# One kernel of four chained layers: layer 2's expert combination taken up in every second round, two products of its keys made by one set of matmuls, and layer 3's weights loaded during layer 2

## The chip, the cores and the metric

The kernel runs on one core of one Trainium2 chip. A core has five engines with a queue each: PE (TensorE: matrix products; the loads of their weights have a row of their own, PEld), DVE (VectorE), ACT (ScalarE), POOL (GpSimd) and SP (SyncE, which here only starts transfers). They meet through semaphores, and each works through its own queue. The metric is the device time of one execution in microseconds (us), as the median of several runs. Beside it there is one profiled execution, from which every instruction's start and duration are known; spans of instructions are taken from that one.

## What is computed

An input of 8 sequences of 512 positions by 128 channels goes through four layers. Each layer normalises x, puts it through an attention-like block (s) and a feed-forward block (ffn), and adds s * silu(ffn) to x. The change touches layers 2 and 3. Cut to what matters:

```python
# layer 2, s: a gated delta rule over positions (4 heads, 32 key and 64 value channels per head)
def _step(S, inp):
    q_t, k_t, v_t, g_t, b_t = inp
    S = S * jnp.exp(g_t)[..., None, None]
    v_eff = (v_t - jnp.einsum('bhk,bhkv->bhv', k_t, S)) * b_t[..., None]
    S = S + k_t[..., None] * v_eff[..., None, :]
    o_t = jnp.einsum('bhk,bhkv->bhv', q_t, S)
    return (S, o_t)
# layer 2, ffn: 8 experts with a capacity of 640 tokens, each token sent to its best two
h = jax.nn.relu(jnp.einsum('ecd,edh->ech', xin, w1) + b1[:, None, :])
out = jnp.einsum('ech,ehd->ecd', h, w2) + b2[:, None, :]
out = out * jnp.where(valid, tok_w, 0.0)[:, :, None]
final = jnp.zeros((S + 1, d), xf.dtype).at[idx.reshape(-1)].add(out.reshape(-1, d))[:S]
# layer 3, s: causal attention, 16 heads of 64, with a position bias; q = x @ Wq and so on, out @ Wo + bo
logits = logits + causal[None, None] + _pos_bias(rel_pos_bias, T)[None]
probs = jax.nn.softmax(logits / dh, axis=-1)
# layer 3, ffn: whole-number weights over 127
h = jax.nn.silu(gate) * up
return jnp.einsum('bsh,dh->bsd', h, wd)
```

## The kernel before

**Order of the work.** The order of PE is written out by hand, by Python generators that are stepped in rounds (`step` takes a generator on to its next `yield`). The instructions of the other engines are put into each queue by the framework that builds the program, which can set an instruction ahead of others that the code writes earlier; dependencies, buffers and semaphores come from it as well. A tile's `tag` names a set of buffers, and `bufs` how many there are; a new tile of a tag waits until the oldest of its buffers is free. Pools are laid on one another: a pool that is opened after another was closed gets its memory.

**Layer 2** (`layer2`, L1043 and on) works on eight units u = 0 to 7 (half of the sequences q, a quarter of the positions t). For each unit four generators run side by side in twelve rounds (`rounds`, L1047): `delta_scan` of u (the recurrence, four chunks of three rounds: pk and rhs; pu and U; pn, po and the new state stn), `delta_inverse` of u + 1 (the triangular inverse of each 32x32 block of key products), `delta_front` of u + 2 (norm, convolution py, scaling, the transposes `chan`) and `delta_output` of u - 1 (named `out`). The inverse makes AT (keys by keys, L1497 to L1507) and PT (keys by queries) from `KT` and the two halves of `chan[1]`, each by 64 groups of 32x32 tiles, and multiplies each by the decay matrix E; AO (POOL, L1515), TT and TM follow from AT, and then four levels of PE products pY and pU.

Beside these run the experts (`experts2`): seven steps each, eight experts, one or two steps in a round, from u = 1 on; they end in round 6 of u = 4. Their outputs go to a DRAM buffer `l2eo_d`. When they are through, `combine2` (L1369) takes the units one by one in two steps. The first loads the unit's s again (`sr`, L1376, from SP), issues eight indirect loads of expert rows (`g<-l2eo_d`, L1311, from POOL: four of the best expert's rows into a tile of tag `xin`, four of the second's into one of tag `eo`, two buffers each) and multiplies both by their weights on DVE (L1384). The second adds them (L1388), takes the tanh on ACT (L1389), multiplies (L1390, L1391) and adds to x on POOL (L1394). It has no PE instruction. It is stepped in every round with u > 3 (L1062). `sr` and the output's `s_sb` (L1676) share the tag `s`, two buffers. Unit 7's combination comes after the last round, as its s is the last to be made.

**Layer 3** (`layer3`, L1684) opens its pools when layer 2's are closed. It loads Wv, Wq and Wk (L194, 512 KB each), the position bias (four DVE memsets L1905 and four loads L1906, 512 KB each), Wo (L194), a small bias (L1695), and the three whole-number weights, which `dequantised` (L1909) turns into transposed floats: a load of 192 KB, a cast (L1917) and a scaling (L1918) on DVE, three PE transposes (L1921) and a copy. All loads are issued by SP. In PE's order the nine transposes stand ahead of layer 3's first own product: the transposes of the first normalised sequence (`ptxnT`), then `pv`, the values from Wv.

The scan step that sets the pace in the later units, in the code's words:

```python
for h in range(4):
    tiles32(pk[:, h, :], r["KT"][:, ch, h, :], st[:, h, :])
...
U = wk.tile([P, 4, 64], F32, tag="U", name=f"U{nm}", bufs=2)
A.copy(U, pu)
...
V.tensor_tensor(new, new, pn, ALU.add)
```

Of the kernel before, what the change touches and what calls it, by code (L numbers as in the profile page):

```python
# [31 lines left out]
def tile_kernel(ctx: ExitStack, tc: tile.TileContext, w: dict, out: bass.AP):  # L32
# [6 lines left out]
    sm = ctx.enter_context(tc.tile_pool(name="sm", bufs=4))  # L39
    fw = sm2 = None  # L40
    keep = ctx.enter_context(tc.tile_pool(name="keep", bufs=1, space=bass.MemoryType.DRAM))
# [985 lines left out]
    def layer2():  # L1027
        nonlocal wk, fw, sm2
        with ExitStack() as lx:
# [9 lines left out]
            with tc.manual_schedule(engines={mybir.EngineType.PE}):  # L1039
                front = delta_front(0, c)  # L1040
                step(front)
                loaded2(c)
                N = 2 * NT  # L1043
                out = iter(())

                def rounds(u, experts, combined, n_experts):
                    nonlocal out  # L1047
                    scan = delta_scan(u, c)
                    inverse = delta_inverse(u + 1, c) if u + 1 < N else iter(())
                    front = delta_front(u + 2, c) if u + 2 < N else iter(())  # L1050
                    for r in range(12):
                        step(scan)
                        step(experts)
                        if not u and r > 1:
                            step(experts)
                        step(inverse)
                        if r > 1:
                            step(front)
                        if r % 3 < n_experts:
                            step(experts)  # L1060
                        step(out)
                        if u > 3:  # L1062
                            step(combined)
                    drain(scan, inverse, front, out)
                    out = delta_output(u, c)

                with tc.tile_pool(name="route2", bufs=1) as rp:
                    routed = route2(rp, c)
                    drain(front)
                    front = delta_front(1, c)  # L1070
                    for _ in delta_inverse(0, c):
                        step(front)
                    drain(front)
                    rounds(0, routed, iter(()), 0)
                    drain(routed)
                with tc.tile_pool(name="ex2", bufs=1) as ep:
                    experts = experts2(ep, c)
                    combined = combine2(ep, c)
                    for u in range(1, N):
                        rounds(u, experts, combined, 1)  # L1080
                    drain(out, experts, combined)

# [320 lines left out]
    def delta_front(u, c):  # L1403
# [20 lines left out]
        for back in range(4):  # L1424
            x = wk.tile([P, 4, P], F32, tag=f"nb{back}", name=f"nb{back}{nm}", bufs=1 if back else 4)
            for s in range(4):
# [11 lines left out]

        y = wk.tile([P, 4, S], F32, tag="y", name=f"y{nm}", bufs=1)
        for ch in range(4):  # L1440
# [34 lines left out]
        for i, parts in enumerate((((0, None, G), (1, gam, V)), ((0, beta, G), (1, None, V)))):  # L1475
            byt = wk.tile([P, 2, 4, 4, 32], F32, tag="byt", name=f"byt{i}{nm}", bufs=1)
            for k, part in enumerate(parts):
                scaled(byt[:, k], *part)
            x = wk.tile([P, 2, 4, 4, 32], F32, tag=f"chan{i}", name=f"chan{i}{nm}", bufs=1 if i else 3)
            V.transpose(x.rearrange("p a c h i -> p (a c h i)"), byt.rearrange("p a c h k -> p (a c h k)"))  # L1480
# [8 lines left out]
    def delta_inverse(u, c):  # L1489
# [6 lines left out]

        prod = []  # L1497
        for i, n in enumerate(("AT", "PT")):
            pp = psS.tile([P, 4, 4, 32], F32, tag="S", name=f"p{n}{nm}")
            for ch in range(4):  # L1500
                for h in range(4):
                    tiles32(pp[:, ch, h, :], r["KT"][:, ch, h, :], chan[1][:, i, ch, h, :])
            x = wk.tile([P, 16, 32], F32, tag=n, name=f"{n}{nm}", bufs=1 + i)
            V.tensor_tensor(x, pp.rearrange("p c h i -> p (c h) i"), E, ALU.mult)
            prod.append(x)
            yield
        AT, r["PT"] = prod  # L1507

# [14 lines left out]
        def flipped(n):  # L1523
            x = wk.tile([P, 16, 32], F32, tag="TM", name=f"TM{nm}_{n}", bufs=1)
            V.transpose(x.rearrange("p n i -> p (n i)"), TT.rearrange("p n i -> p (n i)"))
# [4 lines left out]
        for n in range(1, 5):  # L1530
            pp = psS.tile([P, 16, 32], F32, tag="S", name=f"pY{nm}_{n}")
            for i in range(16):
                tiles32(pp[:, i, :], ao[n][:, i, :], TM[:, i, :])
            Y = wk.tile([P, 16, 32], F32, tag="Y", name=f"Y{nm}_{n}", bufs=1)
            A.copy(Y, pp)
# [50 lines left out]
    def decay_pairs(u, g, c):  # L1586

        gl = wk.tile([P, 16, 32], F32, tag="gl", name=f"gl{u}", bufs=1)
        G.tensor_tensor(gl, bcast(c["leb"], 1, 16), bcast(g, 2, 32), ALU.mult)
        pd = psS.tile([P, S], F32, tag="S", name=f"pd{u}")  # L1590
        mm(pd, c["gt32"], gl.rearrange("p n i -> p (n i)"))
        E = wk.tile([P, 16, 32], F32, tag="E", name=f"E{u}", bufs=1)
        A.activation(E.rearrange("p n i -> p (n i)"), pd, AF.Exp)
# [88 lines left out]
    def layer3():  # L1682
        nonlocal wk
        with ExitStack() as lx:  # L1684
            lp = lx.enter_context(tc.tile_pool(name="l3", bufs=1))
            wk = lx.enter_context(tc.tile_pool(name="wk3", bufs=2))
            c = dict(lp=lp, xnT={}, v={}, qk={}, P={}, PT={}, th={}, s={})
            for n in "vqk":
                c["w" + n] = loaded(lp, [P, 1024], w[f"L3_attn_W{n}"], f"l3w{n}")
            c["bias"] = position_bias(lp, shared["bias"])  # L1690
            c["wo"] = loaded(lp, [P, 8, D], w["L3_attn_Wo"].rearrange("(g p) o -> p g o", p=P), "l3wo")
            G.tensor_scalar(c["wq"], c["wq"], 1.0 / 64.0, 0.0, ALU.mult, ALU.add)
            bo = lp.tile([1, NT, D], F32, name="l3bo")
# [5 lines left out]
            c["one"] = one  # L1699
            c["gT"], c["uT"], c["dT"] = (dequantised(lp, w[f"L3_ffn_w_{n}"], n) for n in ("gate", "up", "down"))  # L1700

# [206 lines left out]

    def dequantised(pool, src, name):  # L1909

        raw = pool.tile([P, 3, P], I32, tag="rawi", name=f"rawi{name}")
        if src.shape[0] == P:
            nc.sync.dma_start(raw, src.rearrange("o (c p) -> o c p", p=P))
        else:
            nc.sync.dma_start(raw, src.rearrange("(c p) d -> p c d", p=P))
        f = pool.tile([P, 3, P], F32, tag="rawf", name=f"rawf{name}")
        V.tensor_copy(f, raw)  # L1917
        V.tensor_scalar(f, f, 1.0 / 127.0, None, ALU.mult)  # L1918
        pt = psS.tile([P, S], F32, tag="S", name=f"pti{name}")
        for k in range(3):  # L1920
            T.transpose(pt[:, k * P : (k + 1) * P], f[:, k, :], ident)  # L1921
        dst = pool.tile([P, 3, P], F32, name=f"l3{name}")
        evac(dst, pt[:, 0 : 3 * P].rearrange("p (c o) -> p c o", o=P))
        return dst

    with tc.tile_pool(name="x12", bufs=1) as x12:
        with tc.tile_pool(name="fw", bufs=8) as fw:
            layers01()
        layer2()
    layer3()  # L1930


# [21 lines left out]
```

## Time and profile before

| | |
|---|---|
| median of 3 runs | 4039.8 us (4029.34 to 4045.39) |
| the profiled execution | 4008.45 us, span 4006.7 us |
| PE busy over the span | 89% |
| layer 2, from its first convolution product to the last s | 2423 to 3161 us |
| layer 3, from its first `pv` to the end | 3192.55 to 4006.7 us |
| granted TensorE clock, mean | 0.933 |
| indirect loads of the combination, `g<-l2eo_d` | 64, of 0.944 us (median) on POOL |

The time is that of one core, so an engine's busy time counts only where the others wait for it. The profile lists, for each idle stretch of an engine, what ended it (the releaser), and follows the chain of work that ended last back from the end. "Issue" stands for time in which an engine waited for nothing that the profile shows. Times in windows are counted from the span's start. In layers 0, 1 and 3 PE is busy in nine tenths of nearly every slice; in layer 2 (slices 24 to 32 of 40) it is busy in four to nine tenths.

### The profile page before, as it was taken

The page shows a single profiled execution, that of the slowest core. Times are in us where ns is not written, and L with a number is a line of the kernel's source. Part 1 is how long each engine was busy: PE and PEld are TensorE (multiplying, and loading weights), DVE is VectorE, ACT ScalarE, POOL GpSimd, SP SyncE. Part 2 cuts the span into 40 slices and gives each one's busy share as a digit, 9 for nine tenths or more (in the row PEclk, how much of TensorE's full clock was granted, in tenths as well). Part 3 has the DMA queues.
Part 4 walks back from the last instruction along what each step waited for, and adds up shares of the span by engine and source line. Part 5 has one row for each costly group of instructions (what it writes and reads, how often), then busy time and mean ns, then how long its engine had stood idle before and what let it go on. Part 6 is the DMA issues. An engine that isn't in the chain of part 4 may idle for free. (4 is left out here: it accounts for less than half of the span.)

```text
span 4006.7 us, 87035 instructions
## 1 busy us (share of the span) xinstructions
PE 3580.8 (89%) x33646; PEld 1712.2 (43%) x33646; DVE 2268.1 (57%) x7301; ACT 1831.8 (46%) x3996; POOL 1470.8 (37%) x2122
## 2 busy tenths in 40 slices
PE   3899999999999999999999985788947599999998
PEld 1343344444344333333333333456635355555555
DVE  4655666665655544446446646544454466666665
ACT  1254454455454556565664641122211155555554
POOL 2233334334443333332333333444373133333333
PEclk6999999999999999999999987899967699999999
DMA  3000000000011232222222320011020200000000
GB/s 110 29 23 30 28 13 30 30 18 26 26 44 51 75 104 72 80 73 72 71 75 68 81 75 28 11 42 51 28 51 22 63 1 4 4 4 4 4 4 6
DMA packets 139420, 163.29 MB, mean 41 GB/s; under 512 B 30047, under 2 KB 79878, under 8 KB 138880
## 3 DMA queue, kind: packets, MB, share of 16 engines
q1 hardware_dynamic: 135680, 150.91, 13.2%
q0 software_dynamic: 3328, 6.82, 1.0%
q8 instruction: 266, 4.36, 0.5%
q14 instruction: 146, 1.20, 0.1%
HBM read 129.94 MB, written 30.08 MB: 40 GB/s over the span
## 5 line engine op out<-in xcount | busy, mean ns | idle before, releaser
L500 DVE CUSTOM_DVE_ANT_0 l0junk<-ps,l0junk 128x512 f32<-128x512 f32 (+3 forms) x1024 | 502.2, 490 | 394.1 <-PE ps L82 319.6
L985 POOL TENSOR_TENSOR h<-h,C 128x512 f32<-128x512 f32 x256 | 325.2, 1271 | 640.1 <-ACT h L983 587.0
L556 ACT ACTIVATE PT<-pt 128x512 f32<-128x512 f32 (+1 forms) x768 | 360.9, 524 | 404.7 <-PE ps L82 364.2
L807 DVE TENSOR_REDUCE nm<-ps 128x1 f32<-128x512 f32 x512 | 331.7, 685 | 327.2 <-PE ps L82 326.2
L1791 POOL TENSOR_SCALAR P<-P,l 128x128 f32<-128x128 f32 (+3 forms) x512 | 262.8, 532 | 537.8 <-DVE l L1789 382.4
L1788 ACT ACTIVATE P<-P,mx 128x128 f32<-128x128 f32 (+3 forms) x512 | 281.2, 550 | 300.0 <-DVE mx L1786 296.5
L82 PE MATMUL ps<-l0kA,l0qA 32*128 32x512 f32 (+3 forms) x2048 | 403.8, 479 | 11.4 <-DVE mx L500 11.4
L560 POOL TENSOR_SCALAR_AFFINE_SELECT PT<-PT 128x256 f32<-128x256 f32 x512 | 202.0, 407 | 518.9 <-ACT PT L556 486.7
L82 PE MATMUL pt<-l0qA,l0kA 32*128 32x512 f32 (+3 forms) x2048 | 373.2, 468 | 2.0 <-DVE nm L807 1.1
L82 PE MATMUL ps<-l1kA,l1qA 32*128 32x512 f32 x1024 | 332.0, 652 | 29.0 <-DVE nm L807 26.7
L845 ACT ACTIVATE PT<-pt 128x512 f32<-128x512 f32 x512 | 276.3, 595 | 176.0 <-PE ps L82 146.3
L82 PE MATMUL av<-PT,vl0v 128*9 128x512 f32 (+3 forms) x3072 | 319.4, 504 | 1.2 <-POOL PT L560 1.2
L82 PE MATMUL ph<-xnT,l1e 128*128 128x512 f32 x512 | 295.4, 660 | 7.2 <-DVE H L834 2.7
L982 ACT ACTIVATE h<-ph 128x512 f32<-128x512 f32 x272 | 162.8, 599 | 252.6 <-PE ph L82 227.0
L82 PE MATMUL pt<-l1qA,l1kA 32*128 32x512 f32 x1024 | 273.6, 644 | 1.0 <-DVE nm L807 1.0
L82 PE MATMUL po<-h,l1e 128*128 128x512 f32 x512 | 266.5, 602 | 0.0
L82 PEld LDWEIGHTS pt<-l0qA,l0kA 32*128 32x128 f32 x2048 | 165.3, 184 | 206.8 <-DVE mx L500 66.9
L1784 DVE CUSTOM_DVE_ANT_0 P<-ps,l3bias 128x128 f32<-128x128 f32 (+3 forms) x512 | 225.0, 486 | 41.2 <-PE ps L82 39.4
L649 POOL TENSOR_TENSOR h<-h,C 128x512 f32<-128x512 f32 x128 | 163.0, 1274 | 112.3 <-ACT h L647 64.3
L647 ACT ACTIVATE h<-ph,l0b 128x512 f32<-128x512 f32 x192 | 132.0, 687 | 127.6 <-PE ph L82 127.5
L82 PEld LDWEIGHTS ps<-l0kA,l0qA 32*128 32x128 f32 x2048 | 158.3, 187 | 48.3 <-DVE mx L500 34.7
L82 PE MATMUL ps<-kT,qT 64*128 64x128 f32 (+3 forms) x1024 | 176.0, 456 | 1.2 <-ACT kT L77 0.7
(522 smaller groups left out, 6424.5 us busy)
## 6 DMA issues: line engine op xcount, KB each, us to landing
C<-wd SPq DMA_DIRECT2D x288, 256.0 KB
qd<-qf SPq DMA_DIRECT2D x24, 256.0 KB
kd<-kf SPq DMA_DIRECT2D x24, 256.0 KB
l0qA<-qd SPq DMA_DIRECT2D x256, 16.0 KB
l0kA<-kd SPq DMA_DIRECT2D x256, 16.0 KB
l2e<-in_L_ffn_w_dram SPq DMA_DIRECT2D x16, 256.0 KB
l3flat<-l3short SPq DMA_DIRECT2D x16, 192.0 KB
l2eo_d<-eo SPq DMA_DIRECT2D x8, 320.0 KB
```

Source lines behind the costliest of these rows:

```text
L82: T.matmul(out_, lhsT, rhs, start=start, stop=stop)
L500: V.tensor_tensor_reduce(c["junk"][:, : (qb + 1) * P], pss[j][:, at], c["mask"][:, (3 - qb) * P :], 1.0, NEG, ALU.add, ALU.max, mx[i][:, q ...
L556: A.activation(p[:, j % 2, :N], pss[j][:, :N], AF.Exp)
L560: G.affine_select(out=own, in_=own, compare_op=ALU.is_ge, fill=0.0, base=0, pattern=[[0, 2], [1, P]], channel_multiplier=-1)
L649: G.tensor_tensor(h, h, C[b, e], ALU.mult)
L807: V.tensor_reduce(nm[g][:, j, qb : qb + 1], pss[j], AX.X, ALU.max, negate=True)
L845: A.activation(Pt[j // 2][:, j % 2, :], pss[j], AF.Exp)
L982: A.activation(h, ph, AF.Relu)
L985: G.tensor_tensor(h, h, C[b, u - u % 2][:, u % 2, :], ALU.mult)
L1784: V.tensor_tensor_reduce(p, src, c["bias"][:, 2 * g + j, (3 - qb) * P :], 1.0, NEG, ALU.add, ALU.max, mx[:, n : n + 1])
L1788: A.activation(p, p, AF.Exp, bias=mx[:, n : n + 1], accum_out=l[:, n : n + 1])
L1791: G.tensor_scalar(p, p, l[:, n : n + 1], 1.0, ALU.mult, ALU.mult)
```

## The change

It has three parts. `combine2` is stepped only in the odd rounds of u > 3. AT and PT are made together: `KT` is the stationary operand of one matmul per tile whose moving operand has both halves of `chan[1]` (64 columns instead of 32), in two halves of eight blocks, each followed by two DVE multiplications of 256 columns instead of one of 512; both products are whole after the second half. And a pool `wk23` (`wf`) is opened around both layers, into which ten of layer 2's tiles move; a generator `weights3`, stepped in every round of u = 7, loads layer 3's seven weights into those tiles' buffers (`y`, `byt`, `chan1`, `gl`, `E`, `nb1`) once layer 2 is through with them, scales Wq, and dequantises into `AT`, `TM` and `Y`. `layer3` takes them from there; the position bias and the small bias are loaded as before. The pool `x12` now stays open during layer 3.

```diff
...
@@ -1042,6 +1042,7 @@
                 loaded2(c)
                 N = 2 * NT
                 out = iter(())
+                weights = weights3()
 
                 def rounds(u, experts, combined, n_experts):
                     nonlocal out
@@ -1059,8 +1060,10 @@
                         if r % 3 < n_experts:
                             step(experts)
                         step(out)
-                        if u > 3:
+                        if u > 3 and r % 2:
                             step(combined)
+                        if u == N - 1:
+                            step(weights)
                     drain(scan, inverse, front, out)
                     out = delta_output(u, c)
 
@@ -1078,7 +1081,7 @@
                     combined = combine2(ep, c)
                     for u in range(1, N):
                         rounds(u, experts, combined, 1)
-                    drain(out, experts, combined)
+                    drain(out, experts, combined, weights)
 
     def masks2(lp):
 
@@ -1422,7 +1425,7 @@
 
         nb = []
         for back in range(4):
-            x = wk.tile([P, 4, P], F32, tag=f"nb{back}", name=f"nb{back}{nm}", bufs=1 if back else 4)
+            x = (wf if back == 1 else wk).tile([P, 4, P], F32, tag=f"nb{back}", name=f"nb{back}{nm}", bufs=1 if back else 4)
             for s in range(4):
                 (G.tensor_copy if s % 2 else A.copy)(x[:, :, 32 * s : 32 * s + 32],
                                                      nT[:, s, 3 - back : P + 3 - back].rearrange("p (c i) -> p c i", i=32))
...
@@ -1473,10 +1476,10 @@
 
         chan = r["chan"] = []
         for i, parts in enumerate((((0, None, G), (1, gam, V)), ((0, beta, G), (1, None, V)))):
-            byt = wk.tile([P, 2, 4, 4, 32], F32, tag="byt", name=f"byt{i}{nm}", bufs=1)
+            byt = wf.tile([P, 2, 4, 4, 32], F32, tag="byt", name=f"byt{i}{nm}", bufs=1)
             for k, part in enumerate(parts):
                 scaled(byt[:, k], *part)
-            x = wk.tile([P, 2, 4, 4, 32], F32, tag=f"chan{i}", name=f"chan{i}{nm}", bufs=1 if i else 3)
+            x = (wf if i else wk).tile([P, 2, 4, 4, 32], F32, tag=f"chan{i}", name=f"chan{i}{nm}", bufs=1 if i else 3)
             V.transpose(x.rearrange("p a c h i -> p (a c h i)"), byt.rearrange("p a c h k -> p (a c h k)"))
             chan.append(x)
         r["KT"], r["QgT"] = chan[0][:, 0], chan[0][:, 1]
@@ -1494,17 +1497,17 @@
         E = decay_pairs(u, r["g"], c)
         yield
 
-        prod = []
-        for i, n in enumerate(("AT", "PT")):
-            pp = psS.tile([P, 4, 4, 32], F32, tag="S", name=f"p{n}{nm}")
-            for ch in range(4):
-                for h in range(4):
-                    tiles32(pp[:, ch, h, :], r["KT"][:, ch, h, :], chan[1][:, i, ch, h, :])
-            x = wk.tile([P, 16, 32], F32, tag=n, name=f"{n}{nm}", bufs=1 + i)
-            V.tensor_tensor(x, pp.rearrange("p c h i -> p (c h) i"), E, ALU.mult)
-            prod.append(x)
-            yield
-        AT, r["PT"] = prod
+        AT = wf.tile([P, 16, 32], F32, tag="AT", name=f"AT{nm}")
+        r["PT"] = wk.tile([P, 16, 32], F32, tag="PT", name=f"PT{nm}", bufs=2)
+        for half in range(2):
+            pp = psS.tile([P, 8, 2, 32], F32, tag="S", name=f"pAP{nm}_{half}")
+            for n in range(8):
+                ch, h = divmod(8 * half + n, 4)
+                tiles32(pp[:, n, :, :], r["KT"][:, ch, h, :], chan[1][:, :, ch, h, :])
+            at = slice(8 * half, 8 * half + 8)
+            for i, x in enumerate((AT, r["PT"])):
+                V.tensor_tensor(x[:, at, :], pp[:, :, i, :], E[:, at, :], ALU.mult)
+            yield
 
         ao = []
 
...
@@ -1684,12 +1687,8 @@
         with ExitStack() as lx:
             lp = lx.enter_context(tc.tile_pool(name="l3", bufs=1))
             wk = lx.enter_context(tc.tile_pool(name="wk3", bufs=2))
-            c = dict(lp=lp, xnT={}, v={}, qk={}, P={}, PT={}, th={}, s={})
-            for n in "vqk":
-                c["w" + n] = loaded(lp, [P, 1024], w[f"L3_attn_W{n}"], f"l3w{n}")
+            c = dict(lp=lp, xnT={}, v={}, qk={}, P={}, PT={}, th={}, s={}, **shared["w3"])
             c["bias"] = position_bias(lp, shared["bias"])
-            c["wo"] = loaded(lp, [P, 8, D], w["L3_attn_Wo"].rearrange("(g p) o -> p g o", p=P), "l3wo")
-            G.tensor_scalar(c["wq"], c["wq"], 1.0 / 64.0, 0.0, ALU.mult, ALU.add)
             bo = lp.tile([1, NT, D], F32, name="l3bo")
             for t in range(NT):
                 nc.sync.dma_start(bo[:, t, :], w["L3_attn_bo"].rearrange("(o d) -> o d", o=1))
@@ -1697,7 +1696,6 @@
             one = lp.tile([1, P], F32, name="l3one")
             G.memset(one, 1.0)
             c["one"] = one
-            c["gT"], c["uT"], c["dT"] = (dequantised(lp, w[f"L3_ffn_w_{n}"], n) for n in ("gate", "up", "down"))
 
             groups = [(b, g) for b in range(B) for g in range(8)]
             n = 2 * len(groups)
@@ -1906,28 +1904,45 @@
             nc.sync.dma_start(bias[:, h : h + 4, 2 * P :], skewed[:, h : h + 4, P - 1 : 3 * P - 1])
         return bias
 
-    def dequantised(pool, src, name):
-
-        raw = pool.tile([P, 3, P], I32, tag="rawi", name=f"rawi{name}")
-        if src.shape[0] == P:
-            nc.sync.dma_start(raw, src.rearrange("o (c p) -> o c p", p=P))
-        else:
-            nc.sync.dma_start(raw, src.rearrange("(c p) d -> p c d", p=P))
-        f = pool.tile([P, 3, P], F32, tag="rawf", name=f"rawf{name}")
-        V.tensor_copy(f, raw)
-        V.tensor_scalar(f, f, 1.0 / 127.0, None, ALU.mult)
-        pt = psS.tile([P, S], F32, tag="S", name=f"pti{name}")
-        for k in range(3):
-            T.transpose(pt[:, k * P : (k + 1) * P], f[:, k, :], ident)
-        dst = pool.tile([P, 3, P], F32, name=f"l3{name}")
-        evac(dst, pt[:, 0 : 3 * P].rearrange("p (c o) -> p c o", o=P))
-        return dst
+    def weights3():
+
+
+        c = shared["w3"] = {}
+        two = wf.tile([P, 2, 1024], F32, tag="y", name="l3wvq")
+        c["wv"], c["wq"] = two[:, 0, :], two[:, 1, :]
+        c["wk"] = wf.tile([P, 1024], F32, tag="byt", name="l3wk")
+        for n in "vqk":
+            nc.sync.dma_start(c["w" + n], w[f"L3_attn_W{n}"])
+        c["wo"] = loaded(wf, [P, 8, D], w["L3_attn_Wo"].rearrange("(g p) o -> p g o", p=P), "l3wo", tag="chan1")
+        names = (("gate", "gT", "gl", "AT"), ("up", "uT", "E", "TM"), ("down", "dT", "nb1", "Y"))
+        raws = []
+        for n, _, tag, _ in names:
+            src = w[f"L3_ffn_w_{n}"]
+            raw = wf.tile([P, NT, P], F32, tag=tag, name=f"l3raw{n}")[:, 0:3, :]
+            nc.sync.dma_start(raw.bitcast(I32), src.rearrange("o (c p) -> o c p", p=P) if src.shape[0] == P else
+                              src.rearrange("(c p) d -> p c d", p=P))
+            raws.append(raw)
+        yield
+        G.tensor_scalar(c["wq"], c["wq"], 1.0 / 64.0, 0.0, ALU.mult, ALU.add)
+        for _ in range(3):
+            yield
+        for raw, (n, key, _, tag) in zip(raws, names):
+            V.tensor_copy(raw, raw.bitcast(I32))
+            V.tensor_scalar(raw, raw, 1.0 / 127.0, None, ALU.mult)
+            yield
+            pt = psS.tile([P, S], F32, tag="S", name=f"pti{n}")
+            for k in range(3):
+                T.transpose(pt[:, k * P : (k + 1) * P], raw[:, k, :], ident)
+            c[key] = wf.tile([P, NT, P], F32, tag=tag, name=f"l3{n}")[:, 0:3, :]
+            evac(c[key], pt[:, 0 : 3 * P].rearrange("p (c o) -> p c o", o=P))
+            yield
 
     with tc.tile_pool(name="x12", bufs=1) as x12:
         with tc.tile_pool(name="fw", bufs=8) as fw:
             layers01()
-        layer2()
-    layer3()
+        with tc.tile_pool(name="wk23", bufs=1) as wf:
+            layer2()
+            layer3()
 
 
 _OUT = (B, S, D)
```

The tiles `y`, `TM`, `Y`, `gl` and `E` are moved from `wk` to `wf` in the same way as `nb1`, `byt` and `chan1` above.

## The prediction

> **What bounds the kernel now.** I read the slices first, to see which stage leaves PE idle, then layer 2 unit by unit, then the waits in its worst unit, then the chain of waits where layer 2 hands over to layer 3. The slices:
>
> ```profile
> PE   3899999999999999999999985788947599999998
> DMA  3000000000011232222222320011020200000000
> ```
>
> Outside layer 2 and its end PE is at 8 or 9 tenths, so the change can only win in slices 24 to 32. Busy times in stretches from one unit's first U to the next one's (units 3, 4, 5, 6, 7), then from the last s product to layer 3's first `pv` (columns: stretch, its length, busy time and instructions of PE, weight loads, DVE, ACT, POOL, granted clock, DMA share, GB/s):
>
> ```profile
> 2783.15:2864.80 81.65, 74.71 (x2112) 54.92 (x2112) 40.64 (x112) 21.05 (x47) 29.45 (x33) 0.92 0.13 36
> 2864.80:2985.18 120.38, 67.52 (x2056) 47.06 (x2056) 57.23 (x141) 19.16 (x44) 83.20 (x95) 0.75 0.24 50
> 2985.18:3065.07 79.89, 59.33 (x2021) 43.66 (x2025) 43.48 (x117) 14.05 (x34) 31.85 (x38) 0.71 0.11 23
> 3065.07:3124.12 59.05, 39.45 (x1944) 33.34 (x1934) 27.36 (x60) 8.20 (x17) 17.35 (x19) 0.70 0.10 22
> 3124.12:3160.60 36.48, 23.92 (x600) 18.08 (x600) 22.04 (x99) 6.31 (x13) 6.67 (x8) 0.83 0.05 17
> 3160.60:3192.55 31.95, 3.54 (x14) 2.36 (x14) 13.11 (x41) 1.07 (x2) 2.95 (x6) 0.50 0.52 166
> ```
>
> Two places stand out. Unit 4 has less for PE than unit 3 (67.52 against 74.71 us) and takes 38.7 us more; POOL goes from 29.45 to 83.20. And in the last stretch PE works 3.54 of 31.95 us. DVE's waits from 2890 to 3000, in which unit 4's end lies (total, times, longest):
>
> ```profile
> DVE g L1384 <- DMA g<-l2eo_d,l2row: 28.1, 7, 6.6
> DVE st L109 <- POOL x L1394: 5.9, 2, 5.3
> DVE un L1459 <- POOL usq L1457: 5.2, 1, 5.2
> DVE g L1384 <- issue: 5.1, 1, 5.1
> ```
>
> DVE stands at the multiplications of gathered rows, and TM and rhs, which PE needs, stand behind them. In the same stretch POOL issues 56 of the 64 gathers, 1.25 us apart (0.94 and 0.30 of issue): 70 us. The second line tells more: `st L109` is layer 3's norm, the last work in the code, and runs in the middle of this burst. So whatever is ready is put into any gap, however late it stands in the code. At the handover the chain of waits reads (start, us, what):
>
> ```profile
> 3160.60 0.70 DVE s_sb L1676
> 3161.32 2.03 DMA l2s_d<-s_sb
> 3163.48 2.65 DMA sr<-l2s_d
> ...
> 3178.35 5.10 DMA rawigate<-in_L_ffn_w_gate_dram
> ...
> 3190.11 0.90 PE ptidown L1921 x3
> 3191.02 0.87 PE ptxnT L125 x4
> 3191.91 0.59 ACT xnT L77
> 3192.55 7.76 PE pv L82 x14
> ```
>
> The last combination ends at 3168.6. Then layer 3's loads queue on SP, the 192 KB weights last, and nine transposes that wait for them stand in PE's order ahead of `ptxnT`.
>
> **The change, part by part. Weights of layer 3.** Nothing that waits for these loads is left ahead of `ptxnT`. It then needs only the normalised sequence. The last x is added by 3168.6, the four memsets L1905 run from 3168.9 to 3173.0, the four `xn` (L118) follow at 3172.95 and take 0.93: 3173.88. Transposes to `pv` took 3190.60 to 3192.55 = 1.95 us; so `pv` starts near 3175.9 instead of 3192.55: **-16.65**. If the memsets went behind `xn` it would be 4 us more. Late next would be the position bias: its four loads were issued 3170.1 to 3171.7, its first use was at 3204.7 and would be at 3188. In the stretch 3170 to 3180 DMA moved 352 and 359 GB/s; 2.1 MB at that rate is 6 us, so it lands by about 3178, 10 us early.
>
> What is added to unit 7: on SP seven issues (0.33 to 0.5 us each), in front of loads and stores of the scan's output; SP was otherwise idle there, and all buffers loaded into were last used by unit 7's front (u = 5) or the start of its inverse (u = 6). On POOL 1.07 us (Wq). On DVE three times 0.36 + 0.36 and one or two copies of 0.56, on ACT the rest (0.48), on PE three times 0.9. Unit 7 waits in turn for PE, DVE and ACT (24 of 36 us PE busy), so a piece in the way costs its length at most: 3 x (0.72 + 0.9) = 4.9 us at worst, 0 if all fall into waits. I take **+2**. The dequantisation was 5.5 us of PE, DVE and copies at the handover; that is in the 16.65. If the raw weights are late, DVE stands there with the scan's rhs behind it: up to 5.1 us (the landing time above) for each of three.
>
> **One set of products.** 128 matmuls of 32 columns took 1.28 us at full clock (`pAT`, 2701.18 to 2702.47), 10 ns each; 32 of 64 columns (`pk`, 3128.32) 0.65 us, 20.3 ns each. Per unit 2 x 1.28 becomes 128 x 20.3 = 2.60: PE's work stays. Half of the instructions go: 1024 matmuls and 1024 weight loads in all. In the chain of waits from 2390 to 3230 "issue" has 9.7% of 840 = 81 us, over some 33,300 PE instructions 2.4 ns each: 2048 x 2.4 = **-5**. (For bounds: PE's idle time by issue ahead of `pPT` is 8.8 us in all, half is 4.4; weight loads' there 18.9, half 9.5; below, 0 if the same fetch is only met later.) The rows are those of the tile `pPT`:
>
> ```profile
> L82 PE MATMUL pPT<-chan,chan x1024: 184/194/258, 2461.0 to 3073.5; 32*32 32x32 f32 x171
>   issue: 18.9, 14
> ```
>
> [...]
>
> DVE gets four multiplications of 256 columns (`stn` L1628, from PSUM too: 0.41) for two of 512 (0.69): 1.64 - 1.38 = 0.26 us, eight times 2.1, half on the path: **+1**. AT is whole only a round later, where PT was before. From AT's end to pY: AO 1.27, TT 1.74, TM 0.70, 0.2 of gaps = 3.9. From PT's end to pY there were 5.3, 24, 8.2, 6.1, 9.6, 7.5, 3.3 and 4.1 us in units 0 to 7, so PE waits longer in unit 6 only (0.6) and has nothing to spare in unit 7: **+1**. Sum of this part -3, from -10 to +3.
>
> **Combination in every second round.** It takes no instruction away: 64 gathers of 1.25 us on POOL, 16 DVE multiplications, all the rest stays. What moves is where they stand in the code: units 0 to 3 were reached in rounds 6, 8, 10 of u = 4 and 0 of u = 5; now in 7, 11, 3 and 7. But the 56 gathers issued by 2992 are all of units 0 to 5 and half of 6 and 7, whose place is u = 6, u = 7 and after the last round: they go when the rows and a buffer are there. Both stay as they were for units 0 to 2. One thing does change by the buffers: tag `s` has two, given in the order of the code, and unit 4's `s_sb` (written at 3027) now comes ahead of unit 3's `sr`. So unit 3's second half leaves the burst, and with it eight gathers whose buffers it frees (four of unit 5, then four of unit 7). Of the last eight, four ran while POOL then waited anyway (1.09 us before `byt` at 2979.4), four held AO back from 2989.5 to 2992.55: 3.0 us; unit 3's `sr` on DVE (0.68) stood ahead of TT. They come back at 3027 and later, where POOL idled 17.6 us. I take **-4**. Bounds: if the burst dissolved, unit 4 would take its PE time and unit 3's idle time, 67.5 + 6.9 = 74.5: -46. If the two multiplications moved to u = 5 each stop DVE for the longest wait seen, 6.6: +13. The value is near the second end, since only an eighth of the gathers moves.
>
> **Sum.** -16.65 + 2 - 3 - 4 = **-21.7 us**, made against the profiled execution: 4008.45 gives 3986.8. That execution is 31 us shorter than the median; taken off the median of 4039.8 it is **4018**. The parts' bounds (loads -20.7 to -1.3 with three late casts; products -10 to +3; combination -46 to +13) leave most between 4000 and 4030.
>
> **Rivals.** *The burst dissolves.* For it: POOL has 40 us free between 3003 and 3100, and a unit's ten us of gathers every four rounds (about 25 us) would fit. Against it: the norm of layer 3 shows that place in the code doesn't hold ready work back. Time: -14.65 - 3 - 46: 3976. *The load's gain is lost to unit 7.* The casts are put where the weights are expected, and DVE stands there with rhs behind: 3 x 5.1 = 15.3 us; -21.7 + 15.3 = -6.4: 4033. For it: DVE did stand seven times for gathers expected earlier. Against: the buffers are free some twenty rounds ahead. *Slower: gathers land on the scan.* If units 3 to 6 move wholly into u = 5 to 7, where PE, DVE and ACT take turns and nothing hides a stop, their eight multiplications stop DVE 6.6 us each: 53, less what the burst loses by it, between 0 and their share of its waits, 4/7 of 28.1 + 5.1 = 19; in the middle +43, with -14.65 and -3 it is +26, or 4066. It decides from 17.65 us of net stops on. For it: the two multiplications outside the burst, at 3045 and 3112, cost DVE 8.9 us more of this wait. Against it: place in the code doesn't hold them, as before. *It doesn't do what it says:* loads are held back by a buffer until the handover; then 16.65 is lost and the sum is -5: 4035. I count this with the second.
>
> **How the numbers follow.** Forecast 0.55 (4005 to 4030), burst dissolved 0.15, gain lost 0.20, gathers on the scan 0.10. A measurement of this kernel tells about 0.5%, 20 us, from no change: 4019.6 is the border, and the forecast lies on it. Of its 0.55 about 0.38 falls beyond, with the first rival's 0.15 that makes faster 0.53; the second and the forecast's rest make no change 0.37; slower 0.10. The range reaches from the dissolved burst to near the slower case: 3974 to 4046.
>
> **What would show it.** `pv` 15 us or more sooner after the last x, with no `pti` between: the loads. First bias use without a wait on DMA: nothing is late next. POOL's gathers still 1.25 us apart for 40 to 48 in a row and DVE's wait for them near 25 us: the burst stands; under 10 us, it dissolved, and the prediction is wrong. `pPT`'s issue waits halved, no new wait of pY for TM in units 2 to 5. Unit 7 longer by more than 5 us would say that the casts come too early.

## The result, and the profile after

| | before | after |
|---|---|---|
| median of the compared runs | 4034.7 us (4 runs, 4029.3 to 4045.4) | 4000.7 us (4 runs, 3994.7 to 4005.5) |
| profiled execution, span | 4006.7 us | 3993.0 us |
| mean granted TensorE clock | 0.933 | 0.935 |

The ratio is 0.9912, 95% interval 0.9884 to 0.9939: faster by 0.9%, 34 us between the medians. Between the two profiled executions only 13.7 us lie; why is the first question below.

The slices of PE and of the DMA engines after:

```profile
PE   3899999999999999999999985689957699999998
DMA  3001000000011232222222211011122100000000
```

The weak slices of PE are the same as before, 24 to 32 of 40. Of the transfers, slice 32 had 2 tenths and has 1; slices 28 to 31 have 6 together instead of 3, as the loads now run during layer 2's last units. The same stretches as before, from one unit's first U to the next one's (units 3, 4, 5, 6, 7), and then from the last s product to layer 3's `pv` (stretch, length, busy time and instructions of PE, weight loads, DVE, ACT, POOL, granted clock, DMA share, GB/s):

```profile
2791.32:2870.21 78.89, 72.56 (x1984) 52.51 (x1985) 40.37 (x115) 21.18 (x47) 27.65 (x32) 0.96 0.12 34
2870.21:2995.22 125.01, 83.00 (x1940) 54.93 (x1944) 55.40 (x143) 19.28 (x43) 78.07 (x88) 0.71 0.20 45
2995.22:3071.23 76.01, 59.02 (x1884) 42.35 (x1878) 44.39 (x131) 14.56 (x35) 37.60 (x45) 0.77 0.24 49
3071.23:3127.45 56.22, 37.68 (x1820) 31.79 (x1810) 26.66 (x59) 8.20 (x16) 18.53 (x20) 0.77 0.18 47
3127.45:3164.47 37.02, 25.59 (x609) 19.25 (x609) 22.97 (x101) 6.79 (x14) 6.67 (x8) 0.82 0.05 17
3164.47:3179.10 14.63, 1.12 (x5) 0.72 (x5) 7.91 (x22) 0.58 (x1) 1.88 (x5) 0.50 0.51 160
```

The last stretch fell from 31.95 to 14.63 us. Unit 4 is still the long one, and longer than in the profile of before (125.01 against 120.38). The chain of waits over the handover after (start, us, what):

```profile
3164.47 0.70 DVE s_sb L1679
3165.19 1.99 DMA l2s_d<-s_sb
3167.32 2.58 DMA sr<-l2s_d
...
3172.66 0.91 DVE l3bias L1903
3173.73 0.91 DVE l3bias L1903
3174.80 0.91 DVE l3bias L1903
3175.88 0.91 DVE l3bias L1903
3176.79 0.34 DVE xn L118 x2
3177.19 1.10 PE ptxnT L125 x4
3178.43 0.59 ACT xnT L77
3179.07 8.85 PE pv L82 x16
```

No load of weights and no `pti` is left in it. What stands there now is the four memsets of the position bias, ahead of the norm.

### The profile page after: what moved, and what is told of

Read it like the earlier page. It is cut to its first block, busy times and chain, and to the rows that moved or that the text cites. A ratio compares the mean times of both kernels' runs of the same rounds, so it can differ in the third digit from the quotient of the medians.

```text
span 3993.0 us, 85015 instructions
## 1 busy us (share of the span) xinstructions
PE 3591.4 (90%) x32622; PEld 1715.4 (43%) x32622; DVE 2260.9 (57%) x7317; ACT 1831.2 (46%) x3996; POOL 1470.6 (37%) x2122
## 3 DMA queue, kind: packets, MB, share of 16 engines
q0 software_dynamic: 3328, 6.82, 1.0%
## 4 chain that ended last, share of the span: by engine, by line
PE 75%; DVE 12%; issue 4%; ACT 3%; POOL 3%; DMA 1%; SPq 1%; POOLq 0%; DVEq 0%; ACTq 0%
PE ph L82 12%; PE pt L82 12%; PE po L82 10%; PE av L82 10%; PE ps L82 7%; PE ptp L1799 3%; PE py L82 3%; PE pk L82 2%; PE s L82 2%; PE pv L82 2%; PE pq L82 2%; ACT P L1786 2%; PE pY L82 1%; PE pU L82 1%; DVE P L1782 1%
## 5 line engine op out<-in xcount | busy, mean ns | idle before, releaser
L82 PE MATMUL ps<-l0kA,l0qA 32*128 32x512 f32 (+3 forms) x2048 | 403.3, 478 | 11.3 <-DVE mx L500 11.3
L82 PE MATMUL av<-PT,v 128*64 128x128 f32 (+3 forms) x1024 | 173.1, 445 | 4.2 <-ACT PT L77 2.5
```

The costliest lines, as they stand in the source:

```text
L82: T.matmul(out_, lhsT, rhs, start=start, stop=stop)
```

## The experiments

Ratios are to the kernel before, on the same chip and in the same runs, with 95% intervals. The stages that the experiments speak of, each from a profiled execution (us; "last x" is the start of the last addition to x on POOL):

| | before | again (e1) | after | e7 | e8 | e9 | e10 | e11 |
|---|---|---|---|---|---|---|---|---|
| unit 1 | 84.8 | 92.0 | 90.8 | 88.8 | 90.1 | 90.1 | 88.9 | 74.1 |
| unit 4 | 120.4 | 130.5 | 125.0 | 78.0 | 94.6 | 73.1 | 79.1 | 73.8 |
| unit 5 | 79.9 | 78.0 | 76.0 | 96.1 | 93.7 | 69.9 | 69.2 | 69.8 |
| unit 6 | 59.1 | 59.4 | 56.2 | 81.1 | 77.9 | 60.0 | 57.0 | 58.5 |
| unit 7 to the last s | 36.5 | 36.6 | 37.0 | 41.8 | 37.2 | 37.8 | 37.0 | 37.6 |
| last x to `pv` | 25.6 | 26.1 | 8.4 | 8.4 | 8.4 | 8.4 | 8.4 | 8.4 |
| layer 2, first `py` to last s | 737.0 | 754.7 | 742.7 | 741.3 | 751.4 | 688.8 | 687.6 | 651.3 |

**e1: the kernel before, unchanged.**

> The kernel before once more, unchanged. The profiled execution of before (4008.45 us) is 26 us below the median of its timed runs (4034.66), that of the changed kernel (3994.69) only 6 below its own (4000.68). If the profiled execution of before was a lucky one: a new profile near 4030 us, ratio 1.00 within 0.3%, and the 20 us more than in the first profile stand in one stage, which its windows show. If a profiled execution is always shorter than a timed one: again near 4008.

4030.7 us, ratio 0.999 [0.9981, 0.9999], span of the profile 4026.7. So a profiled execution is not shorter as such: the first profile of before was low by 20 us, nearly all in layer 2 (737.0 against 754.7), in units 1 and 4. Against this second profile the change gives 17.7 us at the handover and 12.0 in layer 2; with 4 us in other places that is the 33.7 between the spans, and the 34 between the medians.

**e2 to e4: each part alone on the kernel before.** e2 takes the pool `wf` (nine of layer 2's tiles, not ten), `weights3` with its step, and layer 3's use of it; e3 and e4 are these lines:

```diff
-                        if u > 3:
+                        if u > 3 and r % 2:
                             step(combined)
...
+        for half in range(2):
+            pp = psS.tile([P, 8, 2, 32], F32, tag="S", name=f"pAP{nm}_{half}")
+            for n in range(8):
+                ch, h = divmod(8 * half + n, 4)
+                tiles32(pp[:, n, :, :], r["KT"][:, ch, h, :], chan[1][:, :, ch, h, :])
```

> Only the weights of layer 3 are loaded and turned during unit 7; combination in every round, two separate products. Theory: 15 us shorter (17.2 at the handover less 2 for unit 7), ratio 0.996. Rival (the loads hold up unit 7): ratio 0.999 or more, unit 7 longer by 5 to 15 us. If the change's 34 us come from the loads alone: 0.9915.

> Only the combination is stepped in the odd rounds. Theory: the burst of gathers stands, 48 of them in a row instead of 56, time -4 us, ratio 0.999, within 0.997 to 1.001. Rival (the burst dissolves): ratio 0.989, unit 4 near 75 us. Rival (the gathers land on the scan): 1.005 or more.

> Only AT and PT are made by one set of matmuls with 64 columns. Theory: -3 us from fewer instructions, ratio 0.999, within 0.9975 to 1.001, PE's and weight loads' idle time by issue in layer 2 smaller by some 5 us. Rival (cost goes by matmul, not by column): -10 us, 0.9975 or less, a set of 64 matmuls in 0.65 us instead of 1.3. Rival (AT comes too late): +6 us, as unit 1 of the changed kernel was 6 us longer, with pY waiting for TM.

| | time | ratio | of 4034 us |
|---|---|---|---|
| e2, loads | 4015.8 us | 0.9954 [0.9941, 0.9968] | -18.6 |
| e3, combination | 4023.4 us | 0.9975 [0.9963, 0.9987] | -10.1 |
| e4, products | 4028.4 us | 0.9984 [0.9975, 0.9993] | -6.5 |

The parts add up to -35.2 us, the whole has -35.5 (0.88% of 4034). That they meet so closely is partly chance: the unchanged kernel beside them (e1) came out 3.3 us low itself, so some 3 us of each part may be no effect, and e4 is the weakest. In e2 the last x to `pv` fell from 26.1 to 8.4 us, which is nearly all of its gain. The two small gains don't show in the profiles: layer 2 is 755.8 us long in e3 and 755.4 in e4, against 754.7 in e1. That rows and products gain something rests on the timed runs alone; where it lies isn't shown.

**e5: the same effect without the second rounds.** The kernel before, stepping in every round, but holding the combination back in the first half of u = 5, so that unit 3's second half comes behind unit 4's `s_sb`:

```diff
-                        if u > 3:
+                        if u > 3 and (u != 5 or r > 5):
                             step(combined)
```

> The kernel before, with the combination stepped in every round, but not in rounds 0 to 5 of u = 5, so that only units 3 and 4 are put behind the writing of unit 4's s. Theory (the gain of the second-round stepping is that unit 3's second half leaves the burst, by the order in which the buffers of tag s are given): the same as the second-round stepping alone, ratio 0.9975 within 0.0015, 48 gathers before unit 5's first U instead of 56. Rival (the gain comes from the slower stepping of units 0 to 2): ratio 0.999 to 1.000, as the unchanged kernel showed.

4022.2 us, 0.9975 [0.9965, 0.9985]: what e3 has. In both 48 gathers are issued before unit 5's first U (52 in e1, not 56), and unit 4 is 3.4 (e3) and 3.6 us (e5) shorter than in e1. What the second rounds bring is then the order of the two tiles of tag `s`, with unit 3's second half and the gathers behind it, and not the stepping as such.

**e6: the memsets behind the norm.** On the changed kernel:

```diff
-            c["bias"] = position_bias(lp, shared["bias"])
...
                 drain(inputs3(0, c))
+                c["bias"] = position_bias(lp, shared["bias"])
```

> The changed kernel, with the position bias (four DVE memsets and four loads) written behind layer 3's first norm and values in the code. Theory: the first transposes no longer wait for 4.3 us of memsets, the time from the last x to pv falls from 8.4 to about 4.5 us; ratio to before 0.9905 (changed kernel 0.9912). Rival (the bias is late for its first use): DVE's first L1784 waits for the bias's load, ratio 0.992 or more.

The last x to `pv` fell from 8.4 to 4.2 us, as the four memsets' 4 us in the chain above say. The time, 3997.5 us and 0.9912 [0.9896, 0.9927], can't be told from the changed kernel's: 4 us are 0.1%, less than the interval. Shown at its place, not in the total. From `pv` to the end it is 814.0 us, 813.9 after, so the bias isn't late.

**e7 and e8: holding the gathers back.** On the changed kernel, with the combination as its own plan of rounds. In e7 DVE makes the row numbers and the weights from the scan's newest state times zero plus themselves, so no gather and no multiplication can run ahead of its round; in e8 only the weights are made so, and the gathers run when they like.

```diff
+        def late(dst, src):
+            V.scalar_tensor_tensor(dst, c["st"][:, 0, 0:4], 0.0, src, ALU.mult, ALU.add)
...
+            late(ix, sixteen(c["rowf"], k)[:, i, :])
...
+                gathered(g[:, s, :], c["eo_d"], ix[:, s : s + 1])
...
+                late(wt[:, i, :], sixteen(c["wt"], k)[:, i, :])
```

> The changed kernel, with the combination held to its place: the row numbers that each four gathers use and the weights of each unit's multiplication are first made on DVE from themselves and 0 times the scan's state, so neither can be put ahead of the scan; a unit's two sets of gathers are two rounds apart, its multiplication four rounds after the first, one unit every four rounds. Theory (what unit 4 loses, some 50 us, is the burst of gathers run ahead): unit 4 falls from 125 to 80 to 90 us, units 5 to 7 grow by up to 10 in all, ratio to before 0.981 to 0.985. Rival (each gather costs PE its time wherever it stands, or stops the scan where nothing hides it): no better than the changed kernel, 0.991 or more.

> As the one before, but only the multiplications are held to their place; gathers go when a buffer is free. If it is DVE's stop at rows that have not come that costs the time: as the one before, 0.981 to 0.985. If it is POOL's row of gathers with its own work behind: little better than the changed kernel, 0.989 to 0.992. In between, the two shares.

e7: 3997.8 us, 0.9918 [0.9904, 0.9931]. The theory fell. Units 4 to 7 in e7's stretches (columns as above):

```profile
2866.87:2944.83 77.96, 65.57 (x1940) 46.21 (x1944) 36.36 (x100) 16.78 (x39) 32.47 (x36) 0.84 0.12 35
2944.83:3040.90 96.07, 69.86 (x1884) 48.35 (x1878) 53.99 (x153) 15.33 (x36) 53.42 (x62) 0.70 0.18 50
3040.90:3122.04 81.14, 51.18 (x1820) 40.55 (x1810) 42.55 (x102) 9.25 (x19) 46.98 (x52) 0.65 0.27 51
3122.04:3163.86 41.82, 26.45 (x609) 19.82 (x609) 26.56 (x111) 7.32 (x15) 10.51 (x12) 0.79 0.08 21
```

Unit 4 lost its burst and 47 us, as expected; units 5 to 7 took 20, 25 and 5 us more. The price goes along with the gathers. e8 is worse than the changed kernel: 4010.3 us, 0.9944 [0.9930, 0.9958], longer than any time that was expected of it; taking DVE's early stops away is no gain by itself. DVE's waits at the multiplications of gathered rows between 2860 and 3165 (total, times, longest), in the changed kernel and then in e7:

```profile
DVE g L1387 <- DMA g<-l2eo_d,l2row: 16.6, 3, 6.7
DVE g L1387 <- issue: 10.4, 2, 5.3
...
DVE g L1390 <- DMA g<-l2eo_d,ix: 4.7, 3, 3.6
```

In e8 there is no such wait for rows. So e7's 50 us in units 5 to 7 are not DVE's waits for rows, and e8 speaks against them as the burst's price (it also holds the multiplications back behind the scan, which may cost something of its own).

That led back to the trace. PE in the changed kernel, at the start of the burst (start, us, what, idle time ahead and its end):

```profile
2896.73 0.65 PE L82 MATMUL pk<-stn,chan 32*32 32x64 f32 x32
2897.20 0.51 PE L82 MATMUL pY<-TM,AO 32*32 32x32 f32 x35
2898.05 0.27 PE L82 MATMUL pY<-TM,AO 32*32 32x32 f32 x5 [0.34 <-issue]
2898.80 0.24 PE L82 MATMUL pY<-TM,AO 32*32 32x32 f32 x3 [0.49 <-issue]
...
2917.45 0.21 PE L82 MATMUL pY<-TM,AO 32*32 32x32 f32 x1 [1.19 <-issue]
...
2920.30 0.87 PE L82 MATMUL pY<-TM,AO 32*32 32x32 f32 x45 [0.50 <-issue]
2921.10 1.46 PE L82 MATMUL pgw<-g,l2mk 128*128 128x16 f32 x6
2922.40 5.74 PE L82 MATMUL py<-l2wc,nb 128*128 128x512 f32 x8
```

and POOL beside it:

```profile
2897.46 1.02 POOL L1314 DMA_INDIRECT g<-l2eo_d,l2row  x1 [3.17 <-DMA sr<-l2s_d]
2898.79 0.94 POOL L1314 DMA_INDIRECT g<-l2eo_d,l2row  x1 [0.30 <-issue]
...
2916.25 0.94 POOL L1314 DMA_INDIRECT g<-l2eo_d,l2row  x1 [0.30 <-issue]
```

A set of 128 matmuls, 1.29 us at 2884 in the same trace, takes 24 us here. Nothing that the profile shows is waited for; PE goes on by one to six matmuls at a time, some 0.7 us or twice that apart (the stretch's records add up to all 128). It begins with the first of sixteen gathers and ends some 3 us after the last one's issue. The sum of all spaces of over 0.15 us between the starts of two matmuls of one set on 32x32 tiles, where a gather (or the load in its place) was issued in the space or up to 2.5 us ahead of it (us, worked out from the traces). Beside a gather there can also be a space that is there without it, so the last column has all spaces of 0.55 to 0.80 us, near a gather or not, in the first stretch + in the second:

| | 2380 to 2870, by the experts' gathers | 2870 to 3165, by the combination's | all of 0.55 to 0.80 us |
|---|---|---|---|
| before | 16.4 | 15.7 | 1.5 + 2.0 |
| again (e1) | 30.9 | 53.8 | 21.4 + 31.3 |
| after | 30.7 | 60.5 | 22.1 + 35.6 |
| e7 | 31.1 | 50.7 | 23.5 + 27.4 |
| e8 | 33.3 | 51.8 | 23.3 + 29.6 |
| e9 | 31.5 | 0 | 25.9 + 2.8 |
| e10 | 32.9 | 8.6 | 25.3 + 2.2 |
| e11 | 0 | 0 | 0.6 + 0.8 |
| e12 | 11.3 | 16.2 | 0.8 + 2.0 |

Moving the gathers (e7, e8) hardly changes it.

**e9 to e11: as many bytes without gathers.** They leave out the choice of the rows: each load takes 128 consecutive ones.

```diff
-                    gathered(g[:, s, :], c["eo_d"], c["row"][:, i, n : n + 1])
+                    nc.sync.dma_start(g[:, s, :], c["eo_d"][P * (n % 40) : P * (n % 40) + P, :])
```

e10 has `G.dma_start` in its place; e11 is e9 with the experts' `xin` rows loaded by SP as well.

> The changed kernel, but the 64 gathers of the combination are plain loads of 128 rows of 512 bytes each, issued by SP (it leaves out the choice of the rows: the same bytes, buffers and waits, other rows). Theory, new after the last two runs: what the burst costs is neither POOL's queue nor DVE's stop but PE. In the changed kernel's trace PE stands between matmuls of one set, for 0.6 to 0.8 us at a time with no wait in the profile, wherever POOL issues a gather; there are 91 us of such gaps near gathers in layer 2, 60 of them by the combination's. If the gathers as POOL makes them are the cause, unit 4 falls from 125 to 75-82 us with units 5 and 6 at 70-78 and 52-58, the gaps of the combination fall under 10 us, and the ratio to before is 0.979 to 0.983. Rival, DVE's stop at rows and the rows' traffic: the traffic and the multiplications are the same here, so unit 4 stays over 110 us and the ratio at 0.989 to 0.992.

> The changed kernel with the same 64 plain loads (again without the choice of rows), but issued by POOL. If it is POOL's way of making transfers that costs PE, whether indirect or not, the gaps stay (50 to 60 us by the combination), unit 4 is over 100 us or units 5 and 6 grow, and the ratio is 0.986 to 0.994. If only the indirect kind costs, it is as with SP: 0.979 to 0.983 and gaps under 10 us.

> As e9_rows_by_sp, and the 40 gathers of the experts' rows in units 0 to 3 are plain loads by SP too (the choice of these rows is left out as well), so that no gather is left in layer 2. Theory: the rest of the gaps near gathers, some 30 us, goes as well; part of it lies beside other waits, so units 0 to 3 lose 10 to 25 us together and the ratio is 0.973 to 0.980. Rival (the gaps in units 1 to 3 only happen to lie at gathers): units 0 to 3 stay within 4 us of the changed kernel's 105.3, 90.8, 81.4 and 78.9.

e9: 3933.7 us, 0.9760 [0.9747, 0.9774]; e10: 3944.9 us, 0.9790 [0.9776, 0.9803]; e11: 3901.4 us, 0.9678 [0.9665, 0.9691]. The drop is larger than expected in e9 and e11 (in e11 units 0 to 3 together lost 37 us, 356.4 to 319.2, where 10 to 25 were expected); 5 and 6 us of it lie behind all work (809.0 and 808.0 us from `pv` to the end, 813.9 after): from the issue of the last output store to the end there are 9.35 us in every run in which POOL issues 104 transfers, after and e10 among them, 4.41 in e9 with 40 and 3.32 in e11 with none. Up to that issue it is 804.6 us from `pv` after and in e9, 804.7 in e11. Units 4 and 5 of e9:

```profile
2877.89:2950.99 73.10, 58.58 (x1940) 42.85 (x1944) 50.66 (x139) 19.09 (x44) 30.16 (x40) 0.89 0.26 74
2950.99:3020.87 69.88, 54.80 (x1891) 39.50 (x1885) 45.69 (x129) 14.68 (x34) 26.92 (x33) 0.82 0.17 51
```

DVE does the same multiplications and the same bytes arrive, and unit 4 is 52 us shorter: neither the traffic nor the multiplications were the burst's price. Not everything else is equal: a load of one expert's rows needn't wait for the last expert, so 12 of the 64 loads in e9 and e10 start by 2890.2, where the first gather after is at 2897.5. In e10 the bytes come from POOL's queue, with as many packets on the software queue as after (3328 in the whole run), but at less than half the time each:

```profile
2897.59 2.16 POOL L1385 DMA_DIRECT2D g<-l2eo_d  x4 [2.45 <-DVE g L1570]
```

0.54 us each, against 1.25 of an indirect one; the spaces near them fall to 8.6 us, of which few are of the 0.7 us kind (last column: 2.2, as many as without gathers), and layer 2 to 687.6, as with SP. So here it was the indirect kind that cost, not POOL as its issuer. What it is in the indirect kind isn't separated: an indirect load of consecutive rows wasn't run, and POOL's time also went down, from 80 us for the 64 to 34. (With none of it on POOL, in e9, layer 2 is no shorter than with the 34.) In e11 layer 2 is 91 us shorter than after (742.7 to 651.3), and 91 us were the spaces near gathers after (30.7 + 60.5).

That equality must not be read as a proof that every space is lost time. All spaces together, near a gather or not, are 128.4 us after and 63.0 in e11, 65 less. And the first profile of before has 53 us less of such spaces than e1 (32.1 against 84.7), and its layer 2 is only 17.7 us shorter. There the same place reads:

```profile
2897.02 2.02 PE L82 MATMUL pY<-TM,AO 32*32 32x32 f32 x128
...
2928.28 1.98 PE L82 MATMUL pY<-TM,AO 32*32 32x32 f32 x128 [12.69 <-DVE TM L1525]
```

PE gets through its set beside the gathers and then stands for TM, which is behind DVE's waits for rows. The gathers cost much of it either way: through PE's issue, or, where that runs, through rows that come every 1.25 us. How an indirect load holds PE's issue up isn't shown by anything here.

**e12: gathers of half the rows.**

```diff
+                    gathered(g[0:64, s, :], c["eo_d"], c["row"][0:64, i, n : n + 1])
+                    nc.sync.dma_start(g[64:, s, :], c["eo_d"][P * (n % 40) + 64 : P * (n % 40) + P, :])
```

> The changed kernel, but each of the 64 gathers fetches 64 rows instead of 128, and the other 64 rows come by a plain load on SP (their choice is left out). Whole gathers gave 60.5 us of PE's gaps between 2870 and 3165 and 54 us of layer 2; none gave 0 of both. Theory: the cost follows the rows of the gathers, so the gaps near them are 22 to 38 us, layer 2 is 708 to 722 us and the ratio to before 0.982 to 0.986. Rival: it follows the number of gather instructions, whatever is in them; the gaps stay at 50 to 60 us, layer 2 at 733 or more and the ratio at 0.988 or more.

Inconclusive. It ran on another chip, on which the kernel before takes 4007.4 us (4004.1 to 4010.6, 7 runs), where on the three chips of the other experiments it had 4032 to 4034. There it took 3964.9 us, 0.9898 [0.9881, 0.9914], with layer 2 at 705.0. The spaces near its gathers were 16.2 us, but those near the experts' gathers, which the edit leaves alone, were 11.3 too, against 31 to 33 elsewhere. Of 0.55 to 0.80 us there are as few as with no gather at all (e11). So the chips differed in just this cost, and whether it goes by rows or by gathers stays open. A half gather takes POOL nearly as long as a whole one (0.90 against 0.94 us). The first profile of before looks like this chip; whether it was taken there isn't known, and how much the change gives there wasn't measured.

## Why the prediction was right or wrong

It said 4018 us, -21.7 by its sum; 4000.7 came. That is inside its range of 3974 to 4046, though below the 4005 to 4030 of its forecast. The direction was right, and so was what each part does; the sum was short by some 12 to 14 us, spread over three terms of which only the first is sure.

- **Weights of layer 3, -16.65 and +2.** `pv` came 8.4 us after the last x instead of 25.6 or 26.1: -17.2 to -17.7. The memsets stayed ahead of `xn`, as assumed. Late next was nothing: between 3185 and 3200 no wait of DVE is for a DMA. Unit 7 paid 0.5 us (36.5 and 36.6 to 37.0), not 2, so most of the casts seem to fall into waits that were there anyway. Alone the part gave 18.6 us.
- **One set of products, -3.** The mis-sized term is the price of a matmul. The prediction took 20.3 ns from `pk` and so "PE's work stays"; two sets of 64 took 1.09 us each at full clock, 17.0 ns, which makes 2.18 us of 2 x 1.28: 0.38 a unit, 3 in all. The 0.65 us of a set of 32 hold the last matmul's own 0.2 us (`pk`'s median is 214 ns), which a longer set doesn't have more of: from start to start, at full clock, it is 14.0 ns in `pk` and in `pAP` alike, and 8.6 ns with 32 columns (worked out from the traces). So the cost here does not go in proportion to the columns, as the prediction's 2.60 us for 2 x 1.28 had it. The issue term held: idle by issue ahead of these products went from 18.9 + 2.0 to 11.6 us, PE's own share of it from 9.1 to 4.1. (The 18.9 are PE and weight loads together; the prediction's bound took them for the weight loads alone, which have 10.0.) The rows after:

```profile
L82 PE MATMUL pAP<-chan,chan x1024: 211/214/312, 2455.2 to 3076.6; 32*32 32x64 f32 x171
...
  issue: 11.6, 19
```

- **Combination, -4.** Its mechanism, the two buffers of tag `s` that put unit 3's second half and eight gathers behind unit 4's `s_sb`, is what e5 shows; 48 gathers ran up to 2985.3 and eight more came from 3032 on, as stated. Whether the size was wrong is open. The timed runs of e3 have -10.1 (-5 to -15 by the interval), some 3 of which may be no effect; unit 4 is 3.4 us shorter in e3's profile and 3.6 in e5's, about the 4 that were stated (3.0 us of AO and 0.7 of DVE). PE's spaces explain little of the rest: beside the combination's gathers there are 51.6 us of them in e3 and 51.1 in e5, 53.8 in e1, as moved gathers keep theirs.
- **What the burst costs.** The prediction read DVE's waits for rows as the cause, with TM and rhs behind. That is what the profile of before shows, where PE has few of the 0.7 us stops. Where PE has them it isn't the price: e8 has none of these waits and gains nothing, and e9 keeps the multiplications and loses the burst. "The burst dissolves" was priced at -46; e7 dissolved it in unit 4 (-47 us) and gained nothing, since gathers in units 5 to 7 cost them 50 us, near the slower rival's 53. That this size fits is luck: the rival priced DVE's stops at rows, of which e7 has 4.7 us in all, while 50.7 us of PE's spaces moved along with the gathers.
- **The profile and the median.** The step "taken off the median" held, and it was the weakest one: it took a 31 us difference to be outside the change. The profiled execution had few of PE's spaces beside gathers, and so was a low one in the very stage that the change works on. Against its own time the change shows 13.7 us, against a second profile 33.7.

With these stops the granted clock fell too, and the work behind them took longer. After the 24 us above, eight `py` products take 5.74 us, at a granted clock of 0.64 from 2922.4 to 2928.2; in e7 at 3003.2, in a stretch of granted clock 1.00, they take 3.70. The granted clock after is 1.00 from 2880 to 2890, 0.62 from 2897 to 2921, in which PE is busy for 6.55 of 24 us, and 0.65 in the eight us that follow. No single gap of PE in the 24 us is over 1.23 us: what this trace has there is frequent short idles, and the clock fell with them. What sets the clock isn't shown.

## What to carry to other kernels

Before pricing a stage from one profile, look at a second one of the same kernel: where 20 us differ, the stage differs too. Where an engine is said to wait for "issue" inside one uninterrupted set of matmuls, look at what other queues do at that time, before blaming the work that stands nearest; and test a suspected burst by taking its cause away, since moving it only shows whether the price is in the place or in the thing. When a number agrees with a rival's, look whether the wait that the rival names is there too. And what is loaded at a handover may go into the buffers of the stage that is running out: here that cost the stage 0.5 us.

## What the hardware showed unexpectedly

- Beside indirect loads on POOL, PE's issue of small matmuls stopped again and again: 57.7 us of spaces of 0.55 to 0.80 us in layer 2 after, 1.4 without indirect loads (e11). Direct loads from the same queue didn't do it: beside the combination's 2.2 us (e10), against 35.6 after.
- Chips differed in it: 2.8 us of such spaces in e12, and 4007 against some 4033 us for the kernel before.
- On 32x32 tiles a set of 128 matmuls of 32 columns took 10 ns each and one of 64 with 64 columns 17 ns, at full clock; from start to start 8.6 and 14.0 ns.
- The end of the program, behind the last output store's issue, took 9.35 us with 104 transfers issued by POOL, of whichever kind, 4.41 with 40 and 3.32 with none.
